# Layer 3's graph product as seven products of halves in a four-layer graph kernel (fp32, one core)

## The chip, the core and the metric

The kernel runs on one core of a Trainium2 chip. The core has five engines that each follow their own instruction queue: TensorE (PE in the profile, with PEld for its weight loads) multiplies matrices into PSUM; VectorE (DVE) and ScalarE (ACT) work on PSUM and SBUF; GpSimd (POOL) works on SBUF and here issues the output DMAs; SyncE (SP) issues all the other DMAs. The metric is the device time of one launch in microseconds; less is better. All data are fp32.

## The reference

A graph of N = 2708 nodes with D = 512 features per node goes through four layers. Each layer ends in `x = layernorm(x + layer(x))`. Layer 0 is attention with 8 heads over the graph, layer 1 a normalised graph product with a small network, layer 2 a graph attention with additive scores. Layer 3, the one that is changed, is

```python
def _L3_gnn_ref(x, adj, W):
    adj_hat = adj + jnp.eye(n)
    d_inv_sqrt = adj_hat.sum(axis=1) ** (-0.5)
    adj_norm = d_inv_sqrt[:, None] * adj_hat * d_inv_sqrt[None, :]
    return jax.nn.relu(adj_norm @ x @ W)
```

`adj` is 2708 x 2708 of zeros and ones, `W` 512 x 512. Its main cost is the graph product: for every node, the sum of the scaled features of its neighbours.

## The kernel before

Nodes are cut into NC = 22 chunks of P = 128 rows (the last, chunk 21, has 20 rows) and into NB = 6 blocks of BLK = 512 columns (the last, block 5, has 148: chunks 20 and 21). Features are cut into KC = 4 pieces of 128. `X[c]` holds the features of chunk c, `X2[c]` the copy that is kept for the residual sum.

The program is written engine by engine through a tile framework: pools hand out buffers by tag (a pool with `bufs=2` has two per tag, and a third request waits until the first one's readers are done), waits are inserted from the data dependences, and outside layer 0 a list scheduler orders each engine's instructions by the program's order, moving one ahead where another isn't ready yet. Each engine then works through its list strictly in order. The order in which SP issues DMAs is such a list too, so a DMA that waits holds up all DMAs behind it.

At the end of layer 2, block b's finishing steps (`finish2`: column sums, a 512 x 512 product `pf` by `fcw_sb` for each chunk, residual sum and layernorm into `X2[c]`) are a generator that is advanced between the chunks of block b + 1. `scaled(c)` (line 977) then writes `X[c] = X2[c] * rdeg`, the features with the normalisation of the neighbour's side.

Layer 3 before (lines 1013 to 1053): for each block b of output nodes and each chunk m of summed nodes, a 128 x 512 tile of the transposed adjacency is loaded (`load_adjT`, line 533, with the identity added on DVE where the tile crosses the diagonal), and four matmuls (`product`, line 651, recorded under L656) accumulate 128 features each into four PSUM banks `acc`. The stationary operand is `X[m]`, the moving one the adjacency tile. Chunk 21 has only 20 rows: `last_rows` (line 548) copies its four feature pieces to the partitions 0, 32, 64 and 96 of one tile, and the adjacency rows are loaded to the same four places, so that each of its four matmuls has 32 rows of the array to itself. `finish3` copies the four banks into `yt` and, for each chunk of the block, multiplies by `w3_sb` (`mapped`, line 665, recorded under L668 as `pz`), takes the relu with the scale of the node's own side on ACT, adds the residual, normalises and sends the rows out through GpSimd's queue. These steps are advanced after every fourth chunk of the next block. The weights `w3_sb` are loaded into a pool of their own before the first block. The finishing of layer 2's last block falls into layer 3's first block in the same way.

The pools that matter: `atp` with 8 adjacency tiles, `ptp` with 6 tiles of 128 x 512 (layer 2's weights `pt`, unused by layer 3), `ps_acc` with 6 PSUM banks, `ps_m` with 2, `ytp` with 1 buffer of 128 x 4 x 512.

Of the kernel before, what the change touches and what calls it, by code (L numbers as in the profile page):

```python
# [8 lines left out]
F32 = mybir.dt.float32  # L9
AF = mybir.ActivationFunctionType  # L10
ALU = mybir.AluOpType
# [4 lines left out]
P = 128  # L16
BLK = 512
# [5 lines left out]
def kernel(  # L23
# [22 lines left out]
    nc = tc.nc  # L46
    N, D = x.shape
    KD = 64
    NP = wq.shape[1] // P
    KC = D // P  # L50
# [4 lines left out]
    def rows(c):  # L55
        return c * P, min(P, N - c * P)

    def cols(b):
        return b * BLK, min(BLK, N - b * BLK)

    def chunks_of(b):
        n0, w = cols(b)
        return [n0 // P + i for i in range((w + P - 1) // P)]
# [18 lines left out]
    def evac(dst, src, every=2):  # L82
        turn[0] += 1
        if turn[0] % every == 0:
            nc.vector.tensor_copy(dst, src)
        else:
            nc.scalar.copy(dst, src)
# [24 lines left out]
    def load_rows(t, src):  # L112
        nc.sync.dma_start(t, src.rearrange("(k p) f -> p k f", p=P))
# [417 lines left out]
    def groups(m, n):  # L531
        return range(n) if m == NC - 1 else range(1)

    def load_adjT(b, m, name, eye, n):

        n0, w = cols(b)
        m0, mr = rows(m)
        at = atp.tile([P, BLK], F32, tag="at", name=f"at{name}_{b}_{m}")
        if m == NC - 1 and not eye:
            nc.gpsimd.memset(at[:, :w], 0.0)  # L540
        for g in groups(m, n):
            nc.sync.dma_start(at[32 * g : 32 * g + mr, :w], adjT[m0 : m0 + mr, n0 : n0 + w])
            if eye and n0 <= m0 < n0 + w:
                d = at[32 * g : 32 * g + mr, m0 - n0 : m0 - n0 + mr]
                nc.vector.tensor_tensor(d, d, ident[32 * g : 32 * g + mr, 32 * g : 32 * g + mr], ALU.add)
        return at

    def last_rows(t, values, n):

        for g in range(n):  # L550
            nc.sync.dma_start(t[32 * g : 32 * g + LR, :], values[:LR, g * P : (g + 1) * P])
        return t
# [94 lines left out]
    def accs(name):  # L647

        return [ps_acc.tile([P, BLK], F32, tag="acc", name=f"acc{name}_{k}") for k in range(KC)]

    def product(acc, m, values, moving, w, m0=0, m1=NC):

        mr = rows(m)[1]
        for k in range(KC):
            g = 32 * k if m == NC - 1 else 0
            nc.tensor.matmul(  # L656
                acc[k][:, :w],
                last[0][g : g + mr, :] if m == NC - 1 else values[:mr, k * P : (k + 1) * P],
                moving[g : g + mr, :w],
                start=(m == m0),  # L660
                stop=(m == m1 - 1),
            )
# [262 lines left out]

    X2p = ctx.enter_context(tc.tile_pool(name="x2", bufs=1))
    X2 = [X2p.tile([P, D], F32, tag=f"x2_{c}", name=f"x2_{c}") for c in range(NC)]
    ytp = ctx.enter_context(tc.tile_pool(name="ytp", bufs=1))


    if True:
# [45 lines left out]
        def scaled(c):  # L977

            q = rows(c)[1]
            nc.vector.tensor_scalar(X[c][:q], X2[c][:q], rdeg[:q, c : c + 1], None, ALU.mult)  # L980
# [29 lines left out]
    l2.close()  # L1010


    with tc.tile_pool(name="w3p", bufs=1) as w3p, tc.tile_pool(name="zp", bufs=2) as zp:
        w3_sb = w3p.tile([P, KC, D], F32, tag="w3", name="w3_sb")
        load_rows(w3_sb, w3)

        def finish3(b, acc):
            w = cols(b)[1]
            yt = ytp.tile([P, KC, BLK], F32, tag="yt", name=f"yt3_{b}")
            for k in range(KC):  # L1020
                evac(yt[:, k, :w], acc[k][:, :w])
            yield
            for i, c in enumerate(chunks_of(b)):
                r0, q = rows(c)
                pz = mapped(yt, i, q, w3_sb, f"pz{c}")
                z = zp.tile([P, D], F32, tag="z", name=f"z{c}")
                nc.scalar.activation(z[:q], pz[:q, :], AF.Relu, scale=rdeg[:q, c : c + 1])  # L1027
                y = io.tile([P, D], F32, tag="y", name=f"y3_{c}")
                nc.vector.tensor_tensor(y[:q], z[:q], X2[c][:q], ALU.add)  # L1029
                layernorm(y[:q], y[:q], q)  # L1030
                nc.gpsimd.dma_start(out[r0 : r0 + q, :], y[:q])
                yield

        for b in range(NB):
            n0, w = cols(b)
            acc = accs(f"3_{b}")
            for m in range(NC):
                at = load_adjT(b, m, "3", True, KC)
                if b == 0 and m == 14:
                    for _ in fin:  # L1040
                        pass
                    for c in chunks_of(NB - 1):
                        scaled(c)
                    last[0] = last_rows(main.tile([P, P], F32, tag="last", name="lastX3"), X[NC - 1], KC)
                product(acc, m, X[m], at, w)
                if m % 4 == 3:
                    next(fin, None)
            for _ in fin:
                pass
            fin = finish3(b, acc)  # L1050
            next(fin)
        for _ in fin:
            pass

# [44 lines left out]
```

## Time and profile before

| | |
|---|---|
| median of 3 runs | 2653.13 us (2652.56 to 2660.51) |
| the profiled execution | 2662.35 us, of it 2660.6 us span |
| first matmul of layer 3 | 2174.97 us |
| last output DMA issued | 2652.18 us |
| DMA over the span | 384.20 MB, 144 GB/s in the mean |
| ACT, POOL busy | 1231.4 us (46%), 331.8 us (12%) |

The profile is of one execution; its times are us from the span's start. "Busy" counts an engine's instructions and not its waits. A line such as L656 is the line of kernel.py that issued the instruction, often one inside a helper. The "chain of work that ended last" follows the last instruction back, at each step to what released it. The "busy table by stretch" gives each engine's busy time between two moments, with the clock that TensorE was granted (1.00 is full), the mean busy share of the 16 DMA engines and what they moved. The "groups" view sums up instructions of one line and shape. The profiled execution was 9.2 us slower than the median of the runs, so sums over its intervals are set against its own time first.

### The profile page before, as it was taken

The page shows a single profiled execution, that of the slowest core. Times are in us where ns is not written, and L with a number is a line of the kernel's source. Part 1 is how long each engine was busy: PE and PEld are TensorE (multiplying, and loading weights), DVE is VectorE, ACT ScalarE, POOL GpSimd, SP SyncE. Part 2 cuts the span into 40 slices and gives each one's busy share as a digit, 9 for nine tenths or more (in the row PEclk, how much of TensorE's full clock was granted, in tenths as well). Part 3 has the DMA queues.
Part 4 walks back from the last instruction along what each step waited for, and adds up shares of the span by engine and source line. Part 5 has one row for each costly group of instructions (what it writes and reads, how often), then busy time and mean ns, then how long its engine had stood idle before and what let it go on. Part 6 is the DMA issues. An engine that isn't in the chain of part 4 may idle for free.

```text
span 2660.6 us, 41510 instructions
## 1 busy us (share of the span) xinstructions
PE 2599.1 (98%) x15242; PEld 1469.1 (55%) x15242; DVE 1772.1 (67%) x4373; ACT 1231.4 (46%) x2460; POOL 331.8 (12%) x336
## 2 busy tenths in 40 slices
PE   8999999999999999999899999899999999999998
PEld 3445666667676676775456445444444464444445
DVE  2004999999999999999674778986876751111112
ACT  1113878787887878877211002565665430000001
POOL 1110000000000000003210000343433320000000
PEclk9999999999999999999799999999999999999999
DMA  5012888888888888886653444453433122232221
GB/s 196 32 52 70 219 228 208 234 210 220 223 205 234 210 219 228 209 211 144 187 193 91 127 117 138 149 158 107 152 119 92 41 64 73 71 83 78 78 65 42
DMA packets 199613, 384.20 MB, mean 144 GB/s; under 512 B 25161, under 2 KB 34713, under 8 KB 199409
## 3 DMA queue, kind: packets, MB, share of 16 engines
q1 hardware_dynamic: 193104, 364.81, 51.6%
q0 software_dynamic: 6304, 16.74, 1.8%
q8 instruction: 121, 1.98, 0.3%
q14 instruction: 84, 0.68, 0.1%
HBM read 186.36 MB, written 16.73 MB: 76 GB/s over the span
## 4 chain that ended last, share of the span: by engine, by line
PE 76%; issue 10%; DVE 6%; DMA 3%; SPq 2%; ACT 2%; POOL 1%; POOLq 0%; DVEq 0%; ACTq 0%
PE acc L656 20%; PE pss L308 15%; PE av L410 14%; PE acc L762 7%; PE pf L668 3%; PE psv L236 3%; PE psk L209 3%; PE pst L382 3%; PE psq L209 3%; DVE s L316 2%; DVE d L353 1%; PE ph L748 1%; DMA e<-d 1%; PE p L793 1%; PE pz L668 1%
## 5 line engine op out<-in xcount | busy, mean ns | idle before, releaser
L316 DVE CUSTOM_DVE_ANT_0 s<-pss,adj 128x512 f32<-128x512 f32 (+3 forms) x1056 | 594.5, 618 | 29.9 <-PE pss L308 28.6
L338 ACT ACTIVATE s<-s,nm 128x1024 f32<-128x1024 f32 (+1 forms) x528 | 546.3, 1037 | 25.5 <-DVE nm L331 24.5
L308 PE MATMUL pss<-KT,qt 64*128 64x512 f32 (+3 forms) x2112 | 487.2, 568 | 7.3 <-DVE mx L316 7.0
L353 DVE STREAM_TRANSPOSE d<-s 128x1024 f32<-128x1024 f32 (+1 forms) x352 | 416.4, 1221 | 11.0 <-DMA e<-d 4.7
L656 PE MATMUL acc<-at,x 128*128 128x512 f32 (+1 forms) x1008 | 387.2, 542 | 0.0
L656 PE MATMUL acc<-pt,x 128*128 128x512 f32 (+1 forms) x880 | 335.1, 540 | 12.3 <-ACT pt L709 9.7
L410 PEld LDWEIGHTS av<-e,V 128*64 128x64 f32 x5632 | 306.7, 139 | 66.0 <-issue 35.5
L410 PE MATMUL av<-e,V 128*64 128x128 f32 (+1 forms) x5632 | 339.0, 273 | 0.0
L656 PEld LDWEIGHTS acc<-at,x 128*128 128x128 f32 x1008 | 180.8, 190 | 204.9 <-issue 202.4
L308 PEld LDWEIGHTS pss<-KT,qt 64*128 64x128 f32 (+1 forms) x2112 | 198.8, 182 | 154.1 <-issue 73.5
L656 PEld LDWEIGHTS acc<-pt,x 128*128 128x128 f32 x880 | 158.8, 193 | 188.2 <-issue 164.1
L762 PE MATMUL acc<-at,h 128*128 128x512 f32 (+1 forms) x504 | 196.8, 543 | 0.0
L720 POOL TENSOR_TENSOR cs<-cs,pt 128x512 f32<-128x512 f32 (+2 forms) x110 | 156.6, 1424 | 204.6 <-ACT pt L709 197.3
L421 POOL DMA_DIRECT2D otd<-ot x88 | 47.6, 540 | 954.5 <-ACT ot L420 942.1
L93 ACT ACTIVATE ln_t<-lnve 128x1 f32<-128x1 f32 x88 | 17.7, 201 | 312.7 <-DVE lnve L107 312.6
L707 DVE TENSOR_TENSOR pt<-pt,at 128x512 f32<-128x512 f32 (+2 forms) x132 | 107.2, 819 | 75.4 <-ACT pt L706 75.4
L1029 DVE TENSOR_TENSOR y<-z,x 128x512 f32<-128x512 f32 (+1 forms) x22 | 15.2, 692 | 211.2 <-ACT z L1027 211.1
L383 ACT COPY pt<-pst 128x512 f32<-128x512 f32 (+1 forms) x176 | 92.1, 572 | 128.2 <-PE pst L382 128.1
L762 PEld LDWEIGHTS acc<-at,h 128*128 128x128 f32 x504 | 90.2, 190 | 101.4 <-issue 99.2
L1027 ACT ACTIVATE z<-pz,rdeg 128x512 f32<-128x512 f32 (+1 forms) x22 | 15.1, 687 | 259.3 <-PE pz L668 259.3
L410 PEld LDWEIGHTS av<-pt,V 128*64 128x64 f32 x1760 | 93.6, 138 | 69.7 <-ACT adj L172 46.2
L709 ACT ACTIVATE pt<-pt 128x512 f32<-128x512 f32 (+2 forms) x132 | 76.2, 579 | 109.2 <-DVE pt L708 108.9
(170 smaller groups left out, 3035.3 us busy)
## 6 DMA issues: line engine op xcount, KB each, us to landing
e<-d SPq DMA_DIRECT2D x680, 256.0 KB
at<-in_adjT_dram SPq DMA_DIRECT2D x315, 256.0 KB
a<-in_adj_dram SPq DMA_DIRECT2D x38, 677.0 KB
adj<-in_adj_dram SPq DMA_DIRECT2D x42, 512.0 KB
adj<-in_adj_dram SPq DMA_DIRECT2D x21, 330.0 KB
rb<-rs_d SPq DMA_DIRECT2D x44, 128.0 KB
qtd<-qb POOLq DMA_DIRECT2D x21, 256.0 KB, 5.1
qt<-qtd SPq DMA_DIRECT2D x21, 256.0 KB
```

What stands on the lines that cost most here:

```text
L209: nc.tensor.matmul(ps[:, :w], w_sb[:, k, p * P : (p + 1) * P], xb[:, k, :w], start=(k == 0), stop=(k == KC - 1),)
L308: nc.tensor.matmul(pss[j][:q, :hw], qt[j * KD : (j + 1) * KD, p, :q], KT[j * KD : (j + 1) * KD, p, n0 + h0 : n0 + h0 + hw], start=True, st ...
L316: nc.vector.tensor_tensor_reduce(out=s[:q, j, h0 : h0 + hw], in0=pss[j][:q, :hw], in1=a[:q, n0 + h0 : n0 + h0 + hw], scale=1.0, scalar=LOW ...
L338: nc.scalar.activation(self.s[k][:q, j, :w], self.s[k][:q, j, :w], AF.Exp, bias=nm[j][:q], accum_out=smt[c // HALF0][:q, c % HALF0, 2 * p ...
L353: nc.vector.transpose(self.D[k][:b, :, j].rearrange("p i m x -> p m i x"), self.s[k][:b, j, : n * P].rearrange("p (m i x) -> p m i x", i=K ...
L383: nc.scalar.copy(sb[:, :, :q], pt[:, :, :q])
L410: nc.tensor.matmul(self.av[j * KD : (j + 1) * KD, :q], V[:, m, h * KD : (h + 1) * KD], x, start=(self.done == 0), stop=(self.done == NC - 1),)
L656: nc.tensor.matmul(acc[k][:, :w], last[0][g : g + mr, :] if m == NC - 1 else values[:mr, k * P : (k + 1) * P], moving[g : g + mr, :w], sta ...
L668: nc.tensor.matmul(pz[:q, :], yt[:, k, i * P : i * P + q], w_sb[:, k, :], start=(k == 0), stop=(k == KC - 1))
L707: nc.vector.tensor_tensor(pt[:mr, :w], pt[:mr, :w], at[:mr, :w], ALU.subtract)
L720: nc.gpsimd.tensor_tensor(sums[:mr, :w], sums[:mr, :w], pt[:mr, :w], ALU.add)
L762: nc.tensor.matmul(acc[hc][:, :w], lastH[g : g + mr, :] if m == NC - 1 else H[m][:mr, hc * P : (hc + 1) * P], at[g : g + mr, :w], start=(m ...
```

## The change

Strassen's scheme replaces a product of two 2 x 2 block matrices (eight products of blocks) by seven products of sums of blocks. Here the three sizes that are halved are the features (256 and 256), the summed nodes (chunks 0 to 9 and 10 to 19) and the nodes summed for (columns 0 to 1279 and 1280 to 2559). The last 148 nodes, chunks 20 and 21, are done in the plain way in both roles: as output columns (the block of 148, which now comes first) and as summed nodes (`last_shares`).

`combine(m)` makes the seven stationary operands from `X[m]` and `X[10 + m]`: three sums go into buffers that layer 2 no longer needs, two are written over a half of X, two halves are used as they are. Since it overwrites X, it follows the 148-column block's use of the chunk. For each column round (512, 512 and 256 wide), three phases follow: products 5, 2 and 1, then 4 and 7, then 3 and 6, each over 10 pairs of chunks. `edges` loads an adjacency tile (30 tiles a round in each of the last two phases, 20 in the first), `joined` adds or subtracts two of them into a `pt` tile on DVE, and `share` issues two matmuls of 128 features. Results are put together in two `yt` buffers on ACT and DVE. `w3_sb` now takes the buffer of layer 2's `fcw`, which the pf steps read.

```diff
-    ytp = ctx.enter_context(tc.tile_pool(name="ytp", bufs=1))
+    ytp = ctx.enter_context(tc.tile_pool(name="ytp", bufs=2))
...
-    with tc.tile_pool(name="w3p", bufs=1) as w3p, tc.tile_pool(name="zp", bufs=2) as zp:
-        w3_sb = w3p.tile([P, KC, D], F32, tag="w3", name="w3_sb")
-        load_rows(w3_sb, w3)
-
-        def finish3(b, acc):
-            w = cols(b)[1]
-            yt = ytp.tile([P, KC, BLK], F32, tag="yt", name=f"yt3_{b}")
-            for k in range(KC):
-                evac(yt[:, k, :w], acc[k][:, :w])
-            yield
-            for i, c in enumerate(chunks_of(b)):
+    with tc.tile_pool(name="zp", bufs=2) as zp:
+        w3_sb = main.tile([P, KC, D], F32, tag="fcw", name="w3_sb")
+        NH = 10
+        F = D // 2
+        FC = F // P
+        TAIL = NB - 1
...
+        def combine(m):
+
+            x11, x21, x12, x22 = part(m, 0), part(m, 1), part(NH + m, 0), part(NH + m, 1)
+            for name, p0, p1, op in (("1", x11, x22, ALU.add), ("6", x21, x11, ALU.subtract), ("7", x12, x22, ALU.subtract)):
+                t = combined[name, m] = next(slots)
+                nc.vector.tensor_tensor(t, p0, p1, op)
+            nc.vector.tensor_tensor(x21, x21, x22, ALU.add)
+            nc.vector.tensor_tensor(x12, x12, x11, ALU.add)
+            combined["2", m], combined["5", m], combined["3", m], combined["4", m] = x21, x12, x11, x22
+
+        def edges(m, n0, w, name):
+
+            m0, mr = rows(m)
+            at = atp.tile([P, BLK], F32, tag="at", name=f"at3_{name}_{m}")
+            for g in groups(m, KC):
+                nc.sync.dma_start(at[32 * g : 32 * g + mr, :w], adjT[m0 : m0 + mr, n0 : n0 + w])
+            if n0 <= m0 < n0 + w:
+                d = at[:mr, m0 - n0 : m0 - n0 + mr]
+                nc.vector.tensor_tensor(d, d, ident[:mr, :mr], ALU.add)
+            return at[:, :w]
+
+        def joined(a, b, op, name):
+            t = ptp.tile([P, BLK], F32, tag="pt", name=f"j{name}")[:, : a.shape[1]]
+            nc.vector.tensor_tensor(t, a, b, op)
+            return t
...
+        def share(acc, which, m, moving, stop=True):
+            for k in range(FC):
+                nc.tensor.matmul(
+                    acc[k][:, : moving.shape[1]],
+                    combined[which, m][:, k * P : (k + 1) * P],
+                    moving,
+                    start=(m == 0),
+                    stop=(stop and m == NH - 1),
+                )
+
+        def last_shares(accs, starts, n0, w, name):
+
+            for m in (NC - 2, NC - 1):
+                at = edges(m, n0, w, name)
+                mr = rows(m)[1]
+                for k in range(KC):
+                    g = 32 * k if m == NC - 1 else 0
+                    nc.tensor.matmul(
+                        accs[k][:, :w],
+                        last[0][g : g + mr, :] if m == NC - 1 else X[m][:, k * P : (k + 1) * P],
+                        at[g : g + mr],
+                        start=(starts[k] and m == NC - 2),
+                        stop=(m == NC - 1),
+                    )
...
-        for b in range(NB):
-            n0, w = cols(b)
-            acc = accs(f"3_{b}")
-            for m in range(NC):
-                at = load_adjT(b, m, "3", True, KC)
-                if b == 0 and m == 14:
-                    for _ in fin:
-                        pass
-                    for c in chunks_of(NB - 1):
-                        scaled(c)
-                    last[0] = last_rows(main.tile([P, P], F32, tag="last", name="lastX3"), X[NC - 1], KC)
-                product(acc, m, X[m], at, w)
-                if m % 4 == 3:
+        w = cols(TAIL)[1]
+        acc = accs("3_t")
+        order = [m for i in range(NH) for m in (i, NH + i)] + [NC - 2, NC - 1]
+        for i, m in enumerate(order):
+            at = load_adjT(TAIL, m, "3", True, KC)
+            if m == NC - 2:
+                for _ in fin:
+                    pass
+                for c in chunks_of(NB - 1):
+                    scaled(c)
+                last[0] = last_rows(main.tile([P, P], F32, tag="last", name="lastX3"), X[NC - 1], KC)
+                load_rows(w3_sb, w3)
+            product(acc, m, X[m], at, w)
+            if i in (5, 9):
+                next(fin, None)
+            if m >= NH and m < 2 * NH:
+                combine(m - NH)
+        yt = ytp.tile([P, KC, BLK], F32, tag="yt", name="yt3_t")
+        for k in range(KC):
+            nc.scalar.copy(yt[:, k, :w], acc[k][:, :w])
+        fin = finish3(chunks_of(TAIL)[0], len(chunks_of(TAIL)), yt)
+
+        n0 = 0
+        while n0 < NH * P:
+            w = min(BLK, NH * P - n0)
+            n1 = NH * P + n0
...
+            m5, m2, m1 = banks(f"m5_{j}"), banks(f"m2_{j}"), banks(f"m1_{j}")
+            for m in range(NH):
+                b11, b22 = edges(m, n0, w, f"a{j}"), edges(NH + m, n1, w, f"a{j}")
+                both = joined(b11, b22, ALU.add, f"a{j}_{m}")
+                share(m5, "5", m, b22)
+                share(m2, "2", m, b11)
+                share(m1, "1", m, both)
+                if m in (5, 8):
                     next(fin, None)
+            next(fin, None)
+            y0 = ytp.tile([P, KC, BLK], F32, tag="yt", name=f"yt3_{j}a")
+            y1 = ytp.tile([P, KC, BLK], F32, tag="yt", name=f"yt3_{j}b")
+            for k in range(FC):
+                nc.scalar.copy(y1[:, k, :w], m5[k][:, :w])
+            for k in range(FC):
+                nc.scalar.copy(y0[:, FC + k, :w], m2[k][:, :w])
+            for k in range(FC):
+                nc.vector.tensor_tensor(y0[:, k, :w], m1[k][:, :w], y1[:, k, :w], ALU.subtract)
+                nc.vector.tensor_tensor(y1[:, FC + k, :w], m1[k][:, :w], y0[:, FC + k, :w], ALU.subtract)
+
+            def gather(t, *dsts):
+                for dst in dsts:
+                    for k in range(FC):
+                        nc.vector.tensor_tensor(dst[:, k, :w], dst[:, k, :w], t[k][:, :w], ALU.add)
+
+            m4, m7, e = banks(f"m4_{j}"), banks(f"m7_{j}"), banks(f"e0_{j}")
+            for m in range(NH):
+                b21, b11, b22 = edges(NH + m, n0, w, f"b{j}"), edges(m, n0, w, f"c{j}"), edges(NH + m, n1, w, f"c{j}")
+                share(m4, "4", m, joined(b21, b11, ALU.subtract, f"b{j}_{m}"))
+                share(m7, "7", m, joined(b21, b22, ALU.add, f"c{j}_{m}"), False)
+            last_shares(m7 + e, [False] * FC + [True] * FC, n0, w, f"d{j}")
+            next(fin, None)
+            gather(m4, y0, y0[:, FC:])
+            gather(m7, y0)
+            gather(e, y0[:, FC:])
+
             for _ in fin:
                 pass
-            fin = finish3(b, acc)
-            next(fin)
+            fin = finish3(n0 // P, nchunks, y0)
+            m3, m6, e = banks(f"m3_{j}"), banks(f"m6_{j}"), banks(f"e1_{j}")
+            for m in range(NH):
+                b12, b22, b11 = edges(m, n1, w, f"e{j}"), edges(NH + m, n1, w, f"f{j}"), edges(m, n0, w, f"f{j}")
+                share(m3, "3", m, joined(b12, b22, ALU.subtract, f"e{j}_{m}"))
+                share(m6, "6", m, joined(b11, b12, ALU.add, f"f{j}_{m}"), False)
+                if m in (3, 5, 8):
+                    next(fin, None)
+            last_shares(e + m6, [True] * FC + [False] * FC, n1, w, f"g{j}")
...
+            gather(m3, y1, y1[:, FC:])
+            gather(m6, y1[:, FC:])
+            gather(e, y1)
+            fin = finish3(NH + n0 // P, nchunks, y1)
+            n0 += w
```

## The prediction

> **What bounds the kernel now.** Read first the page's busy times and slices (columns as on the page: busy us, share, instructions; then one digit per slice of 66.5 us):
>
> ```profile
> PE 2599.1 (98%) x15242; PEld 1469.1 (55%) x15242; DVE 1772.1 (67%) x4373; ACT 1231.4 (46%) x2460; POOL 331.8 (12%) x336
> ...
> PE   8999999999999999999899999899999999999998
> ...
> DVE  2004999999999999999674778986876751111112
> ```
>
> TensorE is busy throughout; in the last seven slices, layer 3, VectorE (DVE) is nearly idle. Since pipelined matmuls can look busy while they wait, read next the chain of work that ended last, in order of time (start, us, what):
>
> ```profile
> 2135.08 1.03 ACT pt L706 x3
> ...
> 2136.86 5.97 PE acc L656 x32
> ...
> 2147.16 4.03 PE acc L656 x32
> ...
> 2210.12 59.83 PE acc L656 x144
> 2269.95 3.43 PE pz L668 x8
> 2273.39 13.73 PE acc L656 x32
> ```
>
> It is TensorE from end to end, without an engine or a DMA in between, from 2136.86 to 2394.84; after that the view follows the output queue, so the busy table by stretch is needed for the rest:
>
> ```profile
> 1423.00:1673.00 250.00, 249.03 (x737) 121.82 (x738) 179.90 (x428) 30.73 (x71) 0.25 (x1) 1.00 0.49 133
> ...
> 2137.00:2175.00 38.00, 38.00 (x217) 30.04 (x217) 31.77 (x101) 20.22 (x65) 14.62 (x23) 0.96 0.33 83
> ...
> 2270.00:2345.00 75.00, 75.00 (x181) 32.84 (x180) 12.29 (x34) 5.45 (x14) 2.22 (x4) 1.00 0.28 77
> ...
> 2420.00:2495.00 75.00, 75.00 (x181) 32.89 (x180) 10.70 (x30) 4.35 (x11) 1.63 (x3) 1.00 0.29 79
> ```
>
> (Columns after the length: PE, weight load, DVE, ACT, POOL, granted clock, DMA share, GB/s.) Layer 3 is bound by matmul work at full clock, with DMA at 28% and DVE at 15%. Last the groups of layer 3, kept apart by shape (busy us, mean ns):
>
> ```profile
> L656 PE MATMUL acc<-at,lastX 20*128 20x512 f32 x40 | 5.7, 640 | 0.0
> ...
> L1029 DVE TENSOR_TENSOR y<-z,x 128x512 f32<-128x512 f32 x21 | 14.6, 693 | 211.1 <-ACT z L1027 211.1
> ...
> L545 DVE TENSOR_TENSOR at<-at,ident 128x128 f32<-128x128 f32 x21 | 6.0, 291 | 81.6 <-DMA at<-in_adjT_dram 81.6
> ```
>
> **Unit prices.** One matmul of the program is two instructions. In the chain 32 of them take 13.73 us, so a matmul with 512 columns costs 0.858 us, and with 148 columns 4.03/16 = 0.252 us. A line through both gives 0.432 us for 256 columns. The Trainium skill, "FP8 and Floating Point Precision", TensorE Precision Notes, says that true fp32 takes four passes through the array; at 512 columns and 2.4 GHz that is 0.853 us, and the trace agrees. The four matmuls of chunk 21 (20 rows) cost only 5.7/5 = 1.14 us per block instead of 3.43: they lie in different row groups and overlap, as "TensorE: Matmul & The Clock Gate", Part 3, describes; the new code keeps that placement. DVE additions: 0.693 us for 512 columns, 0.291 for 128, so 0.425 for 256; "VectorE: DVE Perf Modes", The TRN2 errata, has (N+151)/0.96 ns for the fp32 tensor_tensor, which gives 0.691 and 0.424.
>
> **TensorE's work.** Before: five blocks of 21 chunks by 4 features = 420 matmuls of 0.858 us. After: a round of 512 columns has 60 (products 5, 2, 1) + 40 (4, 7) + 40 (3, 6) + 8 (chunk 20) = 148; two such rounds and one of 256 columns, at half the price, are 2.5 x 148 = 370. Removed: 50 x 0.858 = **42.9 us**. The small matmuls of chunk 21, the 148-column block, the two pf and the 22 pz steps (3.43 us each) are the same in number. As a test, a block before should last 84 x 0.858 + 1.14 + 4 x 3.43 = 86.9 us; the output DMAs recur every 87.1 us.
>
> **DVE's work, and what hides it.** Per round 50 joins of adjacency tiles, 20 additions out of PSUM and up to 24 diagonal additions; once, 50 additions of feature halves. At w=512 two joins per chunk pair are 1.4 us against 4 matmuls = 3.43 us, so TensorE covers them. In all: joins 2 x 50 x 0.693 + 50 x 0.425 = 90 us, PSUM additions 36, halves 21, diagonals about 11 more: 158 us on top of some 65 in 440 us, about half busy. At the turns of the phases I followed the order of the engines' instructions: the PSUM additions of products 4 and 3 stand ahead of the last 8 matmuls, those of 7, 6 and the rest behind joins made for three more chunk pairs (10 us of matmuls). Cost 0; if that cover failed, 4 additions = 2.8 us at each of 5 turns.
>
> **Layer 2's end.** Thirteen of the 50 additions (5.5 us) are issued among the last weights of layer 2, where DVE is busy 31.77 of 38 us and feeds TensorE. But the four diagonal additions of layer 3, which today make DVE wait for DMAs at 2161 to 2164 ahead of the layer's own work, go away there. Cost 0 (0 to 2).
>
> **The 148-column block, now first.** Set t=0 at its first matmul. TensorE: six chunks at 1.0 us, sums and pf20 to 9.9, four chunks, pf21 to 17.4, ten chunks to 27.5, chunk 20 to 28.5, chunk 21 to 28.8. Before, chunk 21 of the first block was read at 2254.9, 45 us after pf21 had ended (2210.1); now it is due 11 us after. DVE: y, statistics, ACT twice, scaling, 4.0 us in the trace, with four half-additions queued between (1.7 us, and 0.5 us of waits for TensorE's chunks): scaled at about 23.6. SP is in order: four copies of the last rows (0.72 to 0.76 us each in the trace) to 26.7, three small loads to 28.2, and only then the first two tiles of the next phase, issued by 28.9; with 2.4 us to landing (as the output DMAs) and the diagonals, TensorE starts at 31.7 instead of 28.8. Cost **3 us**, from 0 to 7. The idle stretch has a second price: at 2136.86, after 1.05 us of idleness behind small matmuls, 32 instructions took 5.97 us instead of 4.03, with the granted clock down. The skill's TensorE page, Part 1, has the clock fall to half after an idle window of about 3.4 us and return after as long a busy one. I add **1.8 us** (0 to 2). The new 1 MB load of w3 now waits for pf21 to free its buffer, with four tile loads behind it on SP; these are needed from t=25.5 on, 8 us later: cost 0.
>
> **Two waits for a buffer.** There are two yt buffers. In rounds 2 and 3 the second one is held by the previous round's y1 until its last pz, which the order puts after six chunks of product 4; product 7 then waits until ACT has copied product 2 out of its bank (0.59 us plus signals): 0.9 us and 0.7 us, **1.6 us**.
>
> **The end.** The last block now has two full chunks after its PSUM additions (two short ones stand before the first pz) instead of copies: +0.3 us. For unnamed gaps at 12 turns I add 1.0 us.
>
> **DMA.** A tile of 256 KB (rows of 2 KB) is loaded 20 + 31 + 31 times in a round: 21.5 MB, with 2.1 MB of output in 129.3 + 8 x 3.43 = 157 us: 151 GB/s, against 77 before. Inside the loop with products 4 and 7 it is three tiles in 3.43 us, 229 GB/s. Layer 1's stretch had 133 GB/s at a share of 0.49, so such tiles should reach about 271 GB/s; and eight tile buffers plus six joined ones are some three to five chunk pairs in hand. Cost 0. Bounded below by 0; above, if 200 GB/s were all, 7.86 MB would take 39.3 us instead of 34.3, 12 us over 2.5 rounds.
>
> **Sum.** -42.9 + 3.0 + 1.8 + 1.6 + 0.3 + 1.0 = -35.2 us. The profiled execution took 2662.35 us (span 2660.6), so the changed one would take about 2627 there. It lay 9.2 us above the median of the runs, 2653.13; against that the forecast is **2618 us**.
>
> **Rivals.** (a) *Everything hides*: the chain shows that TensorE alone matters, and lastX may arrive in time; 2653.1 - 42.9 = 2610. Against it: the SP order above. (b) *Loads become the bound in the loop of products 4 and 7*: tripled demand speaks for it, the share of 0.28 today against it. At 190 GB/s: 41.4 - 34.3 = 7 us x 2.5 = 17 us, so 2635. (c) *Slower*: the same mechanism with worse rates. The loops with 3, 4, 6, 7 take 195 us of matmuls + 13 pz = 239 us and move 44 MB; the whole gain of 35 us is lost if that lasts 274 us, at 161 GB/s. The decision point is far below the 271 estimated; at 150 GB/s the loss would be 293 - 239 - 35 = 19 us, 2672. (d) *The matmul saving isn't had*, because 256-column matmuls are bound by weight loads: 190 ns each against 216 ns per instruction, and at 148 columns 126 ns per instruction was reached with the same loads. At 0.5 us instead of 0.432, 148 x 0.068 = 10 us: 2628.
>
> **From cases to numbers.** Main case 0.68, (a) 0.11, (b) 0.11, (d) 0.05, (c) 0.03, and 0.02 for a result within the 0.3% (8 us) that the runs (2652.56 to 2660.51) can't tell from none. Faster 0.95, same 0.02, slower 0.03. The range of 8 in 10 runs from 2609 (a, and a little under) to 2634, almost to (b).
>
> **What would show it.** In the changed profile: 50 x 2 fewer matmul instructions of 512 columns' worth; DVE at 4 to 5 tenths in the last slices; DMA share near 0.55; an idle gap of TensorE of about 3 us some 29 us after layer 3's first matmul, ended by a DMA or the diagonal addition, with the clock down after it; two gaps under 1 us ended by ACT's copy of product 2. Wrong would be: TensorE idle behind DMA through the loops of products 4 and 7 (b, c), DVE never resting there, or 256-column instructions spaced over 230 ns (d).

## The result and the profile after

The changed kernel takes **2626.8 us** (median of 6 runs, 2623.72 to 2632.51); the kernel before has 2660.34 (median of 6 runs, 2652.56 to 2661.01, the three shown earlier among them). The ratio is 0.9886, with a 95% interval from 0.9868 to 0.9903: faster by 33.5 us. The forecast was 2618, with a range of 2609 to 2634. Profile against profile, the form in which the forecast was summed, it is 2626.93 against 2662.35, so -35.4 us where -35.2 was predicted. That closeness is luck: in layer 3 itself three terms of the sum were wrong, in both directions, and left -33.3; the other 2.2 us lie ahead of layer 3, as shown below.

First the page's busy times and slices of the changed kernel (columns as before; a slice is now 65.6 us):

```profile
PE 2558.7 (97%) x15298; PEld 1476.8 (56%) x15298; DVE 1907.4 (73%) x4661; ACT 1231.2 (47%) x2464; POOL 332.4 (13%) x336
...
PE   8999999999999999999899999899999999999997
...
DVE  2004999999999999999684678978767775453544
...
DMA  5012888888888888887572444354434213644533
```

VectorE now works 3 to 5 tenths in layer 3 instead of 1 to 2, the loads' share went from about 2 to between 3 and 6, and TensorE is as busy as it was, for 40 us less.

The chain of waits (start, us, what), from the end of the 148-column block into the first round:

```profile
2190.66 9.78 PE acc_t L656 x76
2200.45 2.92 DMA at_a<-in_adjT_dram
2203.73 31.17 PE m L1066 x72
2234.90 3.43 PE pz L668 x8
```

The only step in it that is not TensorE is the load of the first round's tiles, as predicted. The 72 instructions behind it take 31.17 us where 30.9 would be full speed (36 matmuls at 0.858).

The whole of layer 3's waits of TensorE (us in total, times, longest):

```profile
PE m L1066 <- DVE jb L1058: 2.7, 2, 2.4
PE m L1066 <- DVE at_a L1053: 1.3, 1, 1.3
PE m L1066 <- ACT yt_1a L1148: 0.7, 1, 0.7
PE pz L668 <- DVE yt_2b L1156: 0.6, 1, 0.6
PE m L1066 <- ACT yt_2a L1148: 0.5, 1, 0.5
PE m L1066 <- DVE yt_2a L1156: 0.2, 1, 0.2
```

The second line is the predicted gap ahead of the first round, the third and the fifth are the two predicted waits for ScalarE's copy of product 2. The first was not predicted: product 4 waits for a joined tile `jb`. TensorE's timeline at that place (start, us, instructions; the idle time ahead and what ended it in brackets):

```profile
2416.11 8.75 PE L1066 MATMUL m<-jb,x 128*128 128x512 f32 x20
2424.70 1.02 PE L668 MATMUL pz<-w_sb,yt_0b 128*128 128x512 f32 x2
2428.17 3.20 PE L1066 MATMUL m<-jb,x 128*128 128x512 f32 x4 [2.45 <-DVE jb L1058]
2431.15 3.27 PE L668 MATMUL pz<-w_sb,yt_0b 128*128 128x512 f32 x6
2435.10 1.13 PE L1066 MATMUL m<-jc,wc 128*128 128x512 f32 x2 [0.68 <-ACT yt_1a L1148]
```

From 2424.70 to 2435.10, 10.40 us, TensorE does eight `pz` and four product-4 instructions, worth 5.15 us at full speed. Two idle stretches take 3.13 us; in the rest the granted clock is down (0.61 and 0.84, shown further below). This turn loses 5.25 us, and the same turn of the 256-column round 1.15.

The busy table by stretch (length; PE, weight load, DVE, ACT, POOL; clock, DMA share, GB/s): the first round's phases with products 5, 2, 1, then 4 and 7, then 3 and 6:

```profile
2203.73:2262.50 58.77, 58.77 (x136) 25.06 (x137) 20.23 (x47) 4.39 (x10) 1.11 (x2) 1.00 0.50 144
2262.50:2301.40 38.90, 38.90 (x97) 16.84 (x95) 20.21 (x37) 0.00 (x0) 0.00 (x0) 1.00 0.72 213
2301.40:2350.80 49.40, 49.40 (x125) 21.54 (x121) 23.68 (x49) 3.28 (x9) 1.62 (x3) 1.00 0.48 142
```

TensorE is busy all through, at full clock, with VectorE at half and the loads at 0.72 in the heaviest phase. Last, groups by shape:

```profile
L1066 PE MATMUL m<-at_a,x 128*128 128x512 f32 x160 | 72.1, 593 | 1.3 <-DVE at_a L1053 1.3
...
L1066 PE MATMUL m<-at_a,x 128*128 128x256 f32 x80 | 18.9, 379 | 0.0
```

An instruction's own time (593, 379 ns) includes overlap. The starts tell the price: in the timeline eight 256-column instructions follow each other in 1.73 us (2516.70 to 2518.43), 0.216 us each, so 0.432 us for a matmul, as predicted and within 1% of half of the 0.858.

### The profile page after: what moved, and what is told of

Same layout as the page of the kernel before. It is cut to its first block, busy times and chain, and to the rows that moved or that the text cites. A ratio compares the mean times of both kernels' runs of the same rounds, so it can differ in the third digit from the quotient of the medians.

```text
span 2625.1 us, 42264 instructions
## 1 busy us (share of the span) xinstructions
PE 2558.7 (97%) x15298; PEld 1476.8 (56%) x15298; DVE 1907.4 (73%) x4661; ACT 1231.2 (47%) x2464; POOL 332.4 (13%) x336
## 5 line engine op out<-in xcount | busy, mean ns | idle before, releaser
L410 PE MATMUL av<-pt,V 128*64 128x128 f32 (+1 forms) x1760 | 114.3, 276 | 3.6 <-ACT ot L420 3.6
L773 DVE SCALAR_TENSOR_TENSOR cs<-at,rdeg,cs 128x512 f32<-128x512 f32 (+2 forms) x126 | 86.2, 684 | 41.4 <-DMA at<-in_adjT_dram 40.5
L85 DVE COPY KT<-psk 128x512 f32<-128x512 f32 (+1 forms) x12 | 7.5, 628 | 138.5 <-PE psk L209 138.5
```

What stands on the lines that cost most here:

```text
L410: nc.tensor.matmul(self.av[j * KD : (j + 1) * KD, :q], V[:, m, h * KD : (h + 1) * KD], x, start=(self.done == 0), stop=(self.done == NC - 1),)
```

## The experiments

All are measured with one interval of the trace: from the start of the column sums that follow layer 3's first six chunks to the start of the last group of `pz` ("the interval"). Kernels without a stated number of runs had one. The interval leaves out what happens ahead of layer 3, where runs of one kernel differ by several us, and repeats well in the one kernel that was profiled twice: 426.05 us in the changed kernel's first profile, 425.75 in its second.

### A third yt buffer

```diff
-    ytp = ctx.enter_context(tc.tile_pool(name="ytp", bufs=2))
+    ytp = ctx.enter_context(tc.tile_pool(name="ytp", bufs=3))
```

> The changed kernel with three yt buffers instead of two; nothing else. In its own profile the turn into product 7 of the second 512-column round lost 5.25 us of TensorE time (from pz at 2424.70 to product 7 at 2435.10, where 10 instructions of pz and 4 of product 4 needed 5.15) and the same turn of the 256-column round 1.15 us. Theory Y (the buffer is the cause of both): both losses go, layer 3 is 6.4 us shorter, about 2620 us against 2626.8. Rival L (the joined tile came late because the loads or VectorE were late at that turn anyway, the buffer being only the last wait): the 2.4 us wait of product 4 for its joined tile stays, and at most 0.7 + 0.5 us go: 2625 us or more.

Measured: 419.08 us, 7.0 less; 2621.16 us (median of 4 runs, 2617.3 to 2623.99; ratio to before 0.9854, 0.983 to 0.9877). TensorE's waits in layer 3 are now

```profile
PE m L1066 <- DVE at_a L1053: 1.4, 1, 1.4
PE pz L668 <- DVE yt_2b L1156: 0.6, 1, 0.6
```

Both turns run without a stop (the one in the second round holds eight `pz` instructions, not the ten of the expectation's text; 5.15 us is right for eight). Theory Y holds: with the buffer the late joined tile goes too, so the loads and VectorE were not late by themselves.

### The same by order: pz earlier

```diff
-                if m in (5, 8):
+                if m in (3, 5, 7, 9):
                     next(fin, None)
```

> The changed kernel with two yt buffers, but all four final products (pz) of the previous half block issued within the loop of products 5, 2, 1 (after chunk pairs 3, 5, 7, 9 instead of 5, 8 and behind the loop), so that the buffer is free when the copies come. Theory Y: as with a third buffer, layer 3 shorter by 6.4 us, no wait for the copy of product 2. Rival L: the wait for the joined tile stays, 1 us or less is gained.

Measured: 419.54 us, 6.5 less, at no cost in memory; no wait for `jb` or for the copy is left. A wait of 0.3 us for an addition into `yt_2a` stays in the last round (0.2 in the changed kernel). It is the release of the buffer that counts, not the number of buffers.

### Own buffers for product 7's joined tiles

```diff
-            t = ptp.tile([P, BLK], F32, tag="pt", name=f"j{name}")[:, : a.shape[1]]
+            t = (jp if name[0] in "cf" else ptp).tile([P, BLK], F32, tag="pt", name=f"j{name}")[:, : a.shape[1]]
```

(`jp` is a new pool with 6 buffers; `yt` stays at two.)

> The changed kernel with two yt buffers, and six more buffers for joined tiles: those of products 7 and 6 have their own six, so that tiles which wait for product 7 can't hold up those of product 4. Theory Y2 (the buffer wait of some 0.9 us was made 5.25 us long by the joined tiles of product 7 filling the six buffers, so that product 4 starved and the clock fell): product 4 doesn't wait, the turn loses at most 1 us, layer 3 is about 4 us shorter. Rival L (tiles loaded late, the eight load buffers being the limit): the turn still loses 4 us or more. Rival B (the copy alone is the bound): the whole 5.25 us stay, as one wait for the copy.

Measured: 420.86 us, 5.2 less. TensorE's timeline at the same turn:

```profile
2416.39 17.33 PE L1066 MATMUL m<-jb,x 128*128 128x512 f32 x40
2433.55 3.60 PE L668 MATMUL pz<-w_sb,yt_0b 128*128 128x512 f32 x8
2437.83 7.13 PE L1066 MATMUL m<-jc,wc 128*128 128x512 f32 x16 [0.68 <-ACT yt_1a L1148]
```

Product 4 now runs through all ten chunk pairs, and of the stop only the 0.68 us for the copy is left. What held product 4 up in the changed kernel shows in VectorE's timeline there (`at_c` is an adjacency tile, `jb` product 4's sixth joined tile):

```profile
2427.22 0.29 DVE L1053 TENSOR_TENSOR at_c<-at_c,ident 128x128 f32<-128x128 f32 x1 [2.74 <-DMA at_c<-in_adjT_dram]
2427.43 0.69 DVE L1058 TENSOR_TENSOR jb<-at_b,at_c 128x512 f32<-128x512 f32 x1
```

So the chain of causes is: product 7's banks wait for ScalarE's copy, which waits for the `yt` buffer; meanwhile VectorE goes on making product 7's joined tiles, which nobody takes. By 2423.9 five of the six buffers hold one, so that product 4 gets its tiles one at a time; the adjacency tiles are released late in turn, and VectorE stands 2.74 us at a load with product 4's sixth tile next in its list. Then a sixth tile of product 7 takes the last buffer. A wait that alone costs 0.7 us cost 5.25. The edit gives product 7 buffers of its own and makes the joined tiles twelve in all; whether twelve buffers in one common ring would do as well was not tried.

### The first tiles ahead of the last rows

```diff
+                ahead = [edges(0, 0, BLK, "a0"), edges(NH, NH * P, BLK, "a0")]
                 last[0] = last_rows(main.tile([P, P], F32, tag="last", name="lastX3"), X[NC - 1], KC)
```

> The changed kernel with the two adjacency tiles of the first chunk pair of the first round issued ahead of the four copies of the last rows and of the three small loads behind them. Theory: the idle stretch of 1.34 us between the 148-column block and the first round goes, layer 3 is 1.3 us shorter. Rival: the second pair of tiles is late in turn and TensorE waits there instead, 0 to 0.5 us gained; or the last rows, now issued some 0.7 us later, become the wait, and nothing is gained.

Measured: 422.44 us, 3.6 less, but not for the reason given. The wait for `at_a` is gone, yet the first joined tile's matmul starts only 0.4 us earlier after the column sums: the last rows' eight instructions, 0.53 us together before, now stand apart with two instructions of the new round between them, and take 0.93 and 0.51 us. The other 3.2 us come mostly (2.8) from the turn of the second round, which the edit does not touch: the tile was late by 1.35 us instead of 2.45, and the clock stayed up. Why the tile came earlier isn't shown. The two stretches right behind the idle time, the changed kernel's first and this one's second:

```profile
2428.17:2431.15 2.98, 2.98 (x4) 1.20 (x5) 0.29 (x1) 0.00 (x0) 0.00 (x0) 0.61 0.36 88
```

```profile
2422.48:2427.00 4.52, 4.52 (x10) 1.81 (x10) 1.27 (x3) 0.00 (x0) 0.00 (x0) 1.00 0.44 103
```

### Every tile loaded twice

```diff
             for g in groups(m, KC):
                 nc.sync.dma_start(at[32 * g : 32 * g + mr, :w], adjT[m0 : m0 + mr, n0 : n0 + w])
+            if mr == P:
+                t = xl.tile([P, BLK], F32, tag="xl", name=f"xl_{name}_{m}")
+                nc.sync.dma_start(t[:, :w], adjT[m0 : m0 + mr, n0 : n0 + w])
```

(On top of the early `pz`; `xl` has 6 buffers.)

> The kernel of the early pz, in which every full adjacency tile of the three rounds is loaded twice, the second time into a buffer that nobody reads (six buffers of its own). It prices the loads' margin. In the loop of products 4 and 7 it asks for six tiles in 3.43 us, 458 GB/s[...]. Main theory (such tiles reach about 271 GB/s, as estimated before the change): that loop takes 15.7 MB / 0.271 = 58 us instead of 34 to 36, the loop of products 3 and 6 about 58 instead of 52, the 256-column round about 8 more: some 65 us more in all. Rival b (about 190 GB/s is all that loads reach in these loops): 83 us for each of these loops, some 170 us more. If the loads had wide room (400 GB/s): 10 us more or less.

Measured: 418.52 us, 1.0 less than with the early `pz` alone, although 464 MB are moved instead of 410. The 65 and 170 us more that two of the expectation's cases gave did not come, but part of that is the experiment's fault: nothing reads the extra tiles, so the scheduler brought their loads forward: the 60 named `xl_c`, of all three rounds, were issued between 2097.1 and 2329.4 us. What it shows is that loads at 300 GB/s, at a share of 0.92 to 0.96, don't hold TensorE up. The phases 4 and 7, then 3 and 6 of the first round:

```profile
2272.00:2303.00 31.00, 31.00 (x73) 13.71 (x73) 15.28 (x28) 0.00 (x0) 0.00 (x0) 1.00 0.92 300
2307.00:2350.00 43.00, 43.00 (x104) 18.99 (x101) 19.38 (x38) 2.87 (x7) 1.09 (x2) 1.00 0.96 303
```

### The same in lock step

```diff
+                seen = small.tile([P, 1], F32, tag="seen", name=f"seen_{name}_{m}")
+                nc.vector.tensor_tensor(seen, t[:, :1], at[:, :1], ALU.add)
```

> The doubled loads again, but each extra tile is now read once by VectorE (one column, into a scratch tile), so that it can't be loaded far ahead as it was in the first try, where all extra tiles of products 7, 5, 2 and 1 were in by the first round's end and 300 to 324 GB/s cost nothing. Theory (the loads have room up to about 324 / 0.95 = 341 GB/s, no more): in the loop of products 4 and 7 six tiles are due in 3.43 us, 458 GB/s, so it takes 15.7 MB / 0.341 = 46 us instead of 34 to 36, the loop of products 3 and 6 (52 us) hardly changes, and the 256-column round loses 2 to 4: 20 us more than with the early pz, 10 to 30. If 271 GB/s were the limit, 56 us more; if 458 GB/s can be had, under 4 us more (the small reads on VectorE alone).

Measured: 428.22 us, 8.7 more than with the early `pz`; under the theory's 10 to 30, and not where the theory put it, which had 2 to 4 us in the last round and the rest before. After 0.7 us at the very start TensorE doesn't wait in the rounds of 512 columns, at 309 to 370 GB/s in their phases with 4 and 7 and with 3 and 6. All the loss is in the same phases of the last round (256 columns, rows of 1 KB): 2.8 and 6.2 us. The first round's two phases again, and a stretch of the last round:

```profile
2271.00:2303.00 32.00, 32.00 (x76) 14.25 (x75) 15.99 (x41) 0.00 (x0) 0.00 (x0) 1.00 1.01 349
2308.00:2353.00 45.00, 45.00 (x109) 19.91 (x106) 26.08 (x78) 2.87 (x7) 1.08 (x2) 1.00 1.03 370
...
2560.00:2590.00 30.00, 27.27 (x120) 20.63 (x119) 18.64 (x73) 0.41 (x2) 0.54 (x1) 1.00 0.86 244
```

The phase with 4 and 7 would ask for 458 GB/s with all extra tiles in it; it got 349 without holding TensorE up, so the buffers must have spread the rest over the phases beside it. The 213 GB/s of the changed kernel in this phase (233 with the early `pz`) are thus far from what loads of 512 columns can do here. The Trainium skill, "DMA: Bandwidth & Descriptors", Specifications, gives about 358 GB/s as the HBM limit for one core; the highest stretch here, 370, lies above it. In the last round 244 GB/s at a share of 0.86 no longer kept up. VectorE made the joined tiles late there, but not for want of time: in the stretch shown its longest waits are for extra tiles that were still on their way (2.9 us for `xl_e`, 2.4 for `xl_c`). Whether the shorter rows or the order in which it must take the tiles made these loads late was not separated.

### Every joined tile made twice

```diff
             nc.vector.tensor_tensor(t, a, b, op)
+            nc.vector.tensor_tensor(t, a, b, op)
             return t
```

(On top of the early `pz`.)

> The kernel of the early pz, in which VectorE makes each joined tile twice (the second addition writes the same values): 50 more additions of 0.69 or 0.42 us per phase set, 90 us of VectorE time in all. Main theory (VectorE is about half busy in layer 3 and hidden): layer 3 is at most 3 us longer, since in the loop of products 4 and 7 it would then be busy 33 of 37 us. Rival (VectorE's joins already stand close to the bound because they come in order behind waits for tiles and buffers): more than 10 us longer.

Measured: 419.45 us against 419.54: nothing. In the first round's phase with products 4 and 7 VectorE is busy 26 of 31 us and TensorE all of them:

```profile
2267.00:2298.00 31.00, 31.00 (x74) 13.78 (x73) 26.00 (x43) 0.00 (x0) 0.00 (x0) 1.00 0.75 226
```

So the joins are hidden, with room for as many again.

### The last rows by GpSimd, and the half-additions off VectorE

```diff
-            nc.sync.dma_start(t[32 * g : 32 * g + LR, :], values[:LR, g * P : (g + 1) * P])
+            (q or nc.sync).dma_start(t[32 * g : 32 * g + LR, :], values[:LR, g * P : (g + 1) * P])
...
-                last[0] = last_rows(main.tile([P, P], F32, tag="last", name="lastX3"), X[NC - 1], KC)
+                last[0] = last_rows(main.tile([P, P], F32, tag="last", name="lastX3"), X[NC - 1], KC, nc.gpsimd)
```

(On top of the early `pz`.)

> The kernel of the early pz, with the four copies of the last rows issued by GpSimd instead of SyncE, so that the loads of the first round no longer stand behind them. Theory (the order on SyncE's queue makes the 1.3 us gap): no idle stretch of TensorE between the 148-column block and the first round, from the column sums to the last pz 418.2 us instead of 419.5. Rival (the eight load buffers make the first tiles late): the gap stays. Rival 2 (the last rows land later from GpSimd): the wait moves ahead of chunk 21.

Measured: 417.81 us, 1.7 less than with the early `pz` alone. The first round starts 23.3 us after the column sums instead of 24.7, without a wait: the order on SyncE's queue was the cause of that gap, which the kernel with the first tiles ahead could not show cleanly. The second kernel has ScalarE issue these copies, and besides

```diff
-                nc.vector.tensor_tensor(t, p0, p1, op)
+                nc.gpsimd.tensor_tensor(t, p0, p1, op)
```

> As the kernel before it, with the last rows' copies issued by ScalarE, and with the 30 additions of feature halves that write new tiles done by GpSimd instead of VectorE (the 20 in place stay). In two of the runs so far, the ones that reached layer 2's end 4 to 6 us earlier, the chain of waits went over VectorE there, with these additions in it, and TensorE waited 1.4 us for a copy at layer 3's start. Theory: if this run comes early too, that wait is gone or under 0.5 us and layer 3's first six chunks end up to 1.4 us earlier; if it comes late, nothing changes. Rival: GpSimd is so slow in them (some 0.75 us each by its 1.43 us for 512 columns) that product 1 or 3 waits for a half.

Measured: it did reach layer 3 early, and the wait at its start is 0.25 us instead of 1.40. TensorE's 32 instructions at layer 2's end and its first wait in layer 3:

```profile
2129.27 5.97 PE L656 MATMUL acc<-pt,x 128*128 128x148 f32 x32 [1.05 <-ACT pt L709]
...
2168.39 5.80 PE L656 MATMUL acc_t<-at,x 128*128 128x148 f32 x44 [0.25 <-ACT yt L962]
```

against, in the kernel with the early `pz` alone,

```profile
2130.59 4.29 PE L656 MATMUL acc<-pt,x 128*128 128x148 f32 x32 [1.05 <-ACT pt L709]
...
2169.20 5.80 PE L656 MATMUL acc_t<-at,x 128*128 128x148 f32 x44 [1.40 <-ACT yt L962]
```

That does not show that the half-additions caused the 1.40 us. A wait of 1.3 to 1.4 us stands at this place in three profiles (the early `pz`, the tiles ahead, the first doubling of the loads), and these are just the three in which the 32 instructions took 4.29 us. In the ten others with the new order they took 5.96 or 5.97, and none waits more than the 0.25 here; the last rows by GpSimd came early too and had no such wait, with the half-additions on VectorE. So the wait goes with a TensorE that got through layer 2's end 1.7 us faster, and not with an early arrival; what part the half-additions have in it stays open, since this run was not one of the fast three. The interval is 418.80, 1.0 longer than with the last rows by GpSimd, 0.6 of it in a wait for an addition into `yt_2a`; so nothing is won in it.

### The plain product in the new order

```diff
+        for n0 in (0, NH * P, BLK, NH * P + BLK, 2 * BLK, NH * P + 2 * BLK):
+            w = 2 * P if n0 % (NH * P) == 2 * BLK else BLK
+            acc = accs(f"3_{n0}")
+            for m in range(NC):
+                at = edges(m, n0, w, f"p{n0}")
+                product(acc, m, X[m], at, w)
```

> Strassen's products undone, the rest kept: the 148-column block first, w3 in the freed buffer, two yt buffers, and then the same columns in blocks of 512, 512, 512, 512, 256, 256 by the plain product of 22 chunks; no half-additions, no joined tiles. It tells what the products alone save. Theory (50 fewer matmuls at 0.858 us, everything else hidden or counted): column sums to last pz take 417.4 + 42.9 + 1.3 for the gap ahead of the first block, less 0.2 at the end = 461.4 us. Rival (the joins, additions out of PSUM and tripled loads cost time in a spread-out way that no single wait shows): less than 459 us, since plain blocks have none of them. Rival 2 (256-column matmuls cost more than half of a 512-column one): the same on both sides here, so it doesn't show.

Measured: 460.65 us, and 2667.32 in its one run. There is no gap ahead of the first block (0.15 us; one tile is due there instead of two), so the expectation less 1.3 us, 460.1, is met to 0.6. Against the best kernel below it is 43.0 us longer: that is what the products save by themselves, with all joins, additions and loads counted in (42.9 from layer 3's first matmul on, which takes in more of the half-additions). The rival of a spread-out cost is out.

### Both cures, beside the changed kernel

> The changed kernel once more, as the partner of the next two on the same chip. From the column sums after layer 3's first six chunks to the last group of pz: 426.1 us as in its first profile (both theories); its time 2627 us, give or take what happens ahead of layer 3.

> The changed kernel with three yt buffers and the last rows' copies issued by GpSimd: the two cures together. If the turn's stall (7.0 us with its smaller partner) and the gap ahead of the first round (1.3 us and 0.4 us of smaller effects) are independent, column sums to last pz take 417.4 us, 8.7 us less than in the changed kernel, and the time is about 2618. If one cure only moves the wait to the other place: 419 us or more.

The kernel has three `yt` buffers and the last rows by GpSimd. Measured: 417.61 us against 425.75, 8.1 less; the cures add up. By the clock it takes **2621.86 us** (5 runs, 2616.31 to 2624.1; ratio to before 0.9861, 0.984 to 0.9882) beside 2627.94 for the changed kernel on the same chip (4 runs, 2626.65 to 2630.51; 0.9891, 0.9873 to 0.9909) and 2656.13 before (9 runs). The two sets of runs don't overlap; it beats both kernels. TensorE's one wait left in layer 3:

```profile
PE pz L668 <- DVE yt_2b L1156: 0.6, 1, 0.6
```

## Why the prediction was right, and where it was not

Layer 3 from its first matmul to the start of the last `pz` group: 465.57 us before (2174.97 to 2640.54), 432.32 after (2172.78 to 2605.10), so -33.25. The rest of the -35.4 between the two profiles lies ahead of it, in code that the change leaves alone; that it fills the 1.9 us by which the sum missed is luck. Term by term:

| term | predicted | measured |
|---|---|---|
| 50 matmuls fewer | -42.9 | -43.0 (plain product against both cures) |
| gap ahead of the first round | +3.0 | +1.3 |
| clock behind that gap | +1.8 | +0.3 |
| two waits for a yt buffer | +1.6 | +6.4 |
| the end | +0.3 | +0.2 (0.58 against 0.35 of waiting) |
| unnamed | +1.0 | +1.5 (the remainder) |
| layer 3 | -35.2 | -33.3 |

**TensorE's work** was right to 0.1 us, the half price of 256 columns included: rival (d) falls. (The four passes for fp32 that the prediction cites are not tested by any run here; the price itself is.) In the remainder sits something that is not Strassen's: the plain product in the new order takes 466.79 us from layer 3's first matmul, 1.2 more than before, of which 0.3 is one more chunk 21 where a 512-column block is split into two of 256.

**DVE's work at no cost**: right in layer 3, where doubling the joins costs nothing. At layer 2's end it is right in nine of the 12 profiles with half-additions; in the three others TensorE waited 1.3 to 1.4 us, inside the 0 to 2 that was kept, for a cause that stays open.

**The 148-column block**: right in its mechanism, too large in size. With t=0 at layer 3's first matmul, SyncE began the copies at 22.8 (23.6 predicted), the round began at 30.95 (31.7), but the block ended at 29.6, not 28.8: every step of VectorE and SyncE was put a little late and TensorE a little early, and the difference of the two came out less than half as long. The **clock** behind it did not fall. The prediction had taken this price from layer 2's end, where TensorE was idle for 1.05 us amid small matmuls; ahead of the first round 1.34 us of idleness cost at most 0.3 us.

**Two waits for a buffer** is the step that failed: 1.6 predicted, 6.4 measured. The waits themselves were sized well, 0.7 and 0.5 us. What was left out is what stands behind them in the in-order queues: product 7's joined tiles kept the buffers, so product 4's sixth tile came 2.45 us late and the clock fell after that. The order of the instructions, which the prediction had read, had product 4 six pairs ahead of product 7 at this place, and six was also the number of buffers.

**DMA at no cost**: right, but the estimate of 271 GB/s behind it was about a quarter too low. It scaled a share of 0.49 at 133 GB/s up to 1; measured were 324 GB/s at 0.95 in the first doubling and 349 to 370 at a full share in lock step. Rivals (b) and (c), with 190 and 161 GB/s, fall.

**2618 instead of 2627**: the sum was made for the profiled execution and came out at 2627, as measured. Then 9.2 us were taken off because that execution lay above the median of three runs. With three more runs the median before is 2660.34, next to the profiled 2662.35. The correction was scatter: the kernels here that load nothing twice, and are alike or nearly so up to layer 3, reach the column sums between 2174.0 and 2184.8 us, while the interval behind them repeats to 0.3. In the stretch 1673 to 1800 us three of the four earliest of them have a granted clock of 0.99, but the earliest of all has 0.97, and the later ones have 0.95 to 0.97; what decides the arrival was not tried.

**Rival (a)**, everything hides, is nearly what both cures give: with them layer 3 is 41.7 us shorter than before (423.85 against 465.57), of the 43 that the products save.

## What to carry to other kernels

When two products share one ring of staged tiles and one of them has to wait for a buffer, count how many of its staged tiles can pile up: as they fill the ring, the other product gets its tiles one at a time and then none, and a wait of 0.7 us becomes a loss of 5. A ring for each took that loss down to the 0.7 us here (with six more buffers), and freeing the awaited buffer earlier by issuing its last readers sooner took it away altogether, at no cost in memory. And compare kernels over an interval of the trace that holds the change alone: here it repeated to 0.3 us where whole runs of the same kernel scattered over 8.8.

## What was not expected of the hardware

- TensorE's granted clock was 0.61 and 0.84 in the mean of the two 3 us stretches behind an idle time of 2.45 us, and stayed at 1.00 behind 1.34 us (ahead of the first round) and 1.35 us (in the kernel with the tiles ahead). The Trainium skill, "TensorE: Matmul & The Clock Gate", Part 1, speaks of an idle window of about 3.4 us; here 2.45 were enough. The length of the gap alone does not decide: at layer 2's end the same 1.05 us of idleness were followed by 32 instructions in 5.97 us in most profiles and in 4.29 in three, and at layer 3's start the same 44 instructions took 7.48 us behind 1.34 us of idleness in the first doubling of the loads (clock 0.77) and 5.80 behind 1.40 us in the early `pz` (1.00). What else decides was not tried.
- The share of DMA time is no linear scale: 213 GB/s at 0.72, 303 at 0.96, 370 at 1.03. Scaled up from 133 GB/s at 0.49 it gave a limit that was about a quarter too small.
